# A four-layer graph network: z, y and x3 in x2's buffer, scores in the common PSUM banks, layer 3's nodes in the turns' order, bv added to v, whole products for the first four graphs

## The chip, the cores and the metric

One core of one Trainium2 chip runs the kernel. The metric is the device time of one execution in microseconds (us). Engines are named as the profile names them: PE (matrix products), PEld (its weight loads), DVE (vector engine), ACT (scalar engine), POOL (GpSimd), SP (the queue that issues most DMAs).

## The reference: what is computed

128 graphs `x[b]` of 128 nodes and 512 features pass four layers; all share one 128x128 adjacency matrix `adj`. Each layer ends in a residual sum and a layernorm over the features:

```
x1 = LN(x  + relu(max over nodes of adj @ x + b))            layer 0
h  = x1 @ W;  e = leaky_relu(s1_i + s2_j) * adj              layer 1, s1 and s2: h times two vectors
z  = softmax(e) @ h + beta * h
x2 = LN(x1 + elu(z))
x3 = LN(x2 + (adj @ x2) @ W2 + bias2)                        layer 2; the product is called y
q, k, v = x3 @ Wq + bq, x3 @ Wk + bk, x3 @ Wv + bv           layer 3, 8 heads of 64
out = LN(x3 + softmax(q k^T / 8 + mask) @ v)                 mask is -1e9 where adj is 0
```

Everything is float32.

## The kernel before: how the work is laid out

**Steps.** PE's work is cut into small steps per graph: `l0` (adj times x), `zT` (the attention matrix plus beta, times x1, transposed), `z` (times W), `yT` and `y` (the same for layer 2), `q`, `k`, `v`, `sc` (scores, one product per head) and `avT` (weights times v, transposed). The last six graphs (LATE) take another way at the end (`pT`, `av`), and the first four (EARLY) transpose on PE what the others transpose by DMA.

**Products in seven parts.** Two graphs (for z and y) or four (for q, k, v) are multiplied by a weight in seven products of blocks instead of eight, with sums of weight blocks (`weight_sums`, once) and differences of data blocks (`turned` for z and y, `token_sums` for q, k and v, on POOL). The seven steps of one product (`l1_seven`, `l2_seven`, `seven`) use three PSUM banks: *chain*, *first* and *pair*. Between the steps ACT copies the chain out into a temporary (`stz`, `sty`, `st`), and DVE adds it to what the other banks hold (`finish`; L610 for z, L721 for y, L878 for q, k and v). For y, POOL adds x2 to the temporary (L713).

**Turns.** A transpose of 128x128 blocks is done in `turn` (L373): the tile is written to device memory in four blocks, read back with blocks and rows exchanged, and DVE transposes 32x32 blocks (L393 in place for the softmax weights, L397 into another tile). The read gives the node order 32 x 4, so L397 writes with a step of four elements to restore it. x3 is turned for q, k and v (`turn_x`), the attention matrix (`turn_att`), the softmax weights (`turn_pr`) and the result of avT (`turn_o`). ACT's copy L1047 writes oT with a step of four as well, in both versions.

**Layer 3's last part.** `fetch` (L785) reads x3 back from device memory, in the copy that the turn wrote there, and POOL adds bv to it (L796). After turn_o, POOL multiplies by 1/denominator (L1060), adds x3 plus bv (L1061), and `last` makes the layernorm (L360, L362 on DVE, L365, L367, L369 on POOL, L371 on ACT) and writes the graph out.

**The order of the work.** `Plan` runs at build time: a model of the engines in which each piece of work has a cost in us written in the code, and marks for what must be done first. `run` takes PE's steps in the order of their `place` (turn of the graph plus an offset per step: l0 0, zT and z 2, yT and y 5, sc 14.5, av 17.5) among those that are ready in the model and find their buffers. The other engines' instructions are emitted when the model gives them to their engine, first ready first emitted. Every engine's queue, SP's included, then runs in the order of emission. HOP is the model's time from one engine to the next.

**Buffers.** x1 has five tiles of a graph, x2 four, xp four (for z, for y and x3, for the result), x3r one (for x3 read back), pr (the softmax weights) one. PSUM has eight banks: six under the tag mm for all products, and one tile of two banks, `sc`, for the scores. In `l3_scores` one DVE addition of mask and scores (L974) reads both banks.

Of the kernel before, what the change touches and what calls it, by code (L numbers as in the profile page):

```python
# [14 lines left out]
P = 128  # L15
# [4 lines left out]
HOP = 0.2  # L20


class Plan:

# [9 lines left out]
    def __init__(self, bufs):  # L34
        self.heap, self.count = [], 0
        self.engine = {}
        self.left = dict(bufs)
        self.parked = {tag: [] for tag in bufs}
        self.marks, self.waiting = {}, {}
        self.end = 0.0  # L40
# [35 lines left out]
    def events(self, until):  # L76
        while self.heap and self.heap[0][0] <= until:
# [13 lines left out]
            gen, (engine, us, landing) = item  # L91
            start = max(time, self.engine.get(engine, 0.0))
            self.engine[engine] = start + us
            self.end = start + us + landing + HOP
            self.resume(gen, self.end)
# [43 lines left out]
def kernel(  # L139
# [30 lines left out]
        "x0": 2, "x1": 5, "x2": 4, "x3r": 1, "xp": 4,  # L170
        "s2_bc": 2, "s2_row": 2, "e": 2, "pe": 2, "att": 1, "attT": 2, "zyT": 2, "Tzy": 1,
        "xTh": 3, "T": 1, "st": 3, "stzy": 2, "qTh": 3, "kTh": 3, "pr": 1, "pT": 1, "oT": 1,
        "turn1": 2, "turn4": 2,
    }
    ps_bufs = {"mm": 6, "sc": 1}
# [11 lines left out]
    def ps_tile(tag, name):  # L187
        shape = [P, 2, H // 2, P] if tag == "sc" else [P, 512]
        return psum.tile(shape, F32, tag=tag, name=name, bufs=ps_bufs[tag])
# [12 lines left out]
    def dve(us):  # L202
        return ("DVE", us - 0.09, 0.09)

    def act(us):
        return ("ACT", us - 0.1, 0.1)

    def pool(us):
        return ("POOL", us, 0.0)

    def sp(us, landing):
        return ("SP", us, landing)
# [12 lines left out]
    def load_w(w, name):  # L225
        return const.tile([P, NCC, C], F32, tag=name, name=name), w.rearrange("(c p) f -> p c f", p=P)

# [16 lines left out]
    for c in range(NCC):  # L244
# [9 lines left out]
        load_w(w, f"{n}_sb") for n, w in (("w2", w2), ("wq", wq), ("wk", wk), ("wv", wv))  # L254
# [3 lines left out]
    def later_loads():  # L258

        for us, dst, src in (  # L260
# [4 lines left out]
            yield act(0.16)  # L265
            nc.scalar.dma_start(out=dst, in_=src)
# [19 lines left out]
    nc.vector.tensor_scalar(mask, adj_sb, 0.0, NEG, ALU.is_equal, ALU.mult)  # L286
    mask_bc = mask.rearrange("p (b c) -> p b c", b=NQ).unsqueeze(1).to_broadcast([P, H, NQ, Q])
# [5 lines left out]
    def w1_a():  # L293

        yield sp(0.0, 6.5)
        for i in (1, 0):
# [18 lines left out]
            yield ("PE", 1.0, 0.0)  # L315
# [15 lines left out]
    def weight_sums(n, w):  # L331
# [4 lines left out]
        yield sp(0.0, {"z": 0.0, "y": 30.0, "q": 44.0, "k": 52.0, "v": 84.0}[n])  # L336
# [4 lines left out]
        if n == "z":  # L341
            yield ("mark", ("wa", 0))
# [14 lines left out]
    def layernorm(src, dst, name):  # L357
        yield dve(0.86)
        stats = small.tile([P, 6], F32, tag="stats", bufs=5, name=f"stats_{name}")
        nc.vector.bn_stats(stats, src)  # L360
        mv = small.tile([P, 2], F32, tag="mv", bufs=5, name=f"mv_{name}")
        nc.vector.bn_aggr(mv, stats)  # L362
        yield pool(1.09)
# [6 lines left out]
        yield act(0.82)  # L370
        nc.scalar.activation(dst, src, AF.Identity, bias=nmr, scale=rstd)  # L371

    def turn(src, tag, place, n, name, kept="turn_hbm{}"):  # L373
# [4 lines left out]

        kept = kept.format(n)
        d = yield from get_hbm(kept, [NQ, P, n * Q], f"turn_hbm_{name}")  # L380
        yield sp(0.35, {1: 4.0, 4: 5.5, 8: 5.5}[n])
        nc.sync.dma_start(out=d.rearrange("b p x -> p b x"), in_=src.rearrange("p b n r -> p b (n r)"))
        plan.give(tag)
        t = yield from get("pT" if place is None else f"turn{n}", [P, NQ, n, Q], f"turn_{name}")
# [4 lines left out]
        if kept.startswith("turn"):  # L389
            plan.give(kept)  # L390
        if place is None:
            yield dve(1.25)
            nc.vector.transpose(t.rearrange("p a n c -> p (a n c)"), t.rearrange("p a n c -> p (a n c)"))  # L393
            return t
        dst = yield from place()
        yield dve({1: 0.4, 4: 1.11}[n])
        nc.vector.transpose(dst.rearrange("p n (c a) -> p a n c", a=NQ), t)  # L397
        plan.give(f"turn{n}")
        return d
# [66 lines left out]
    def attention(b, s2_bc, tag):  # L466
# [26 lines left out]
        yield from turn(att.rearrange("p (b n c) -> p b n c", b=NQ, n=1), "att", lambda: made(s["attT"]), 1, f"att_{b}")  # L493
# [21 lines left out]
    def turned(n, b, ps):  # L515
# [10 lines left out]
        if j == 0:  # L526
            return
# [3 lines left out]
        for i, dst, x_, y_ in ((0, t[:, 0], b12, b11), (1, t[:, 1], b22, t[:, 0]), (2, b12, b22, b12), (3, t[:, 2], b21, t[:, 1])):  # L531
            yield pool(0.8)
# [20 lines left out]
    def pair_products(n, t):  # L553

        p, i = divmod(t, 7)
        d = pairs[n, p]
# [14 lines left out]
        if t == 7 * (B // 2) - 1:  # L571
# [3 lines left out]

    def pair_waits(n):
        def waits(t):
            p, i = divmod(t, 7)
            keys = [("sums", n)]
# [14 lines left out]
    def l1_seven(t):  # L594
# [3 lines left out]
        def half(j, r):  # L598
            return st[2 * p + j]["xp1"][:, r * HALF : (r + 1) * HALF]

        def temp():
            d["st", i] = yield from get("stzy", [P, HALF], f"stz_{p}_{i}")
            yield act(0.37)
# [3 lines left out]
        def finish(j, r, key):  # L607
            yield ("mark", ("z", p, key))
            yield dve(0.42)
# [4 lines left out]
        def take_xp(j):  # L614
            st[2 * p + j]["xp1"] = yield from get("xp", [P, C], f"xp1_{2 * p + j}")
# [3 lines left out]
        elif i == 1:  # L619
            yield from take_xp(0)  # L620
            yield from finish(0, 0, 0)
            plan.give("mm")
        elif i == 4:
            yield from temp()
            yield from take_xp(1)
            yield from finish(1, 1, 4)
        elif i == 5:
            yield ("mark", ("z", p, "C", 1, 1))
            yield act(0.37)
# [8 lines left out]
    def l1_rest(b):  # L638
        s = st[b]
        xp = s.pop("xp1")  # L640
        x2 = yield from get("x2", [P, C], f"x2_{b}")
        yield act(1.25)
        nc.scalar.activation(x2, xp, AF.Relu, scale=-1.0)
        nc.scalar.activation(x2, x2, AF.Exp, scale=-1.0)
        yield dve(1.5)
        nc.vector.scalar_tensor_tensor(xp, xp, 0.0, s.pop("x1"), ALU.max, ALU.add)  # L646
        nc.vector.scalar_tensor_tensor(xp, x2, -1.0, xp, ALU.add, ALU.add)  # L647
        plan.give("x1")
        yield from layernorm(xp, x2, f"1_{b}")
        plan.give("xp")  # L650
        s["x2"] = x2
# [21 lines left out]
    def token_sums(g):  # L673
# [8 lines left out]
        for i, dst, x_, y_ in ((0, t[:, 0], b12, b11), (1, t[:, 1], b22, t[:, 0]), (2, b12, b22, b12), (3, t[:, 2], b21, t[:, 1])):  # L682
            yield pool(1.4)
# [5 lines left out]
    def l2_seven(t):  # L689
# [3 lines left out]
        def half(j, r, tile):  # L693

            return st[2 * p + j][tile][:, r * HALF : (r + 1) * HALF]

        def xp_half(j, r):
            xp, b = st[2 * p + j]["xp2"], 2 * p + j
            if b < EARLY:
                return xp[:, r * HALF : (r + 1) * HALF]  # L700
# [489 lines left out]
```

## Time and profile before

| what | value |
|---|---|
| median of 3 runs | 2791.49 us (2790.95 to 2792.59) |
| the profiled execution | 2791.27 us |
| its span, first to last instruction | 2789.5 us |
| mean granted clock of PE | 0.988 |
| DMA | 392.58 MB in 459820 packets, 376624 of them under 2 KB |

The profile is one execution. A page lists the busy time of each engine; other views give windows of the span, a timeline, the waits, and groups of instructions by line. PE's matmuls are pipelined and their ends modelled, so the durations in the timeline overlap: the next start tells more than the duration. A wait is put down to the last of its releasers by the profile.

### The profile page before, as it was taken

To read this page: it belongs to the slowest core of one execution; us is meant where nothing else is said; L and a number is where in the kernel's file an instruction comes from. 1 tells how busy PE (TensorE), PEld (TensorE's weight loads), DVE (VectorE), ACT (ScalarE), POOL (GpSimd) and SP (SyncE) were. 2 spreads that over 40 slices of the span, in tenths; PEclk is the share of its full clock that TensorE was granted. 3 is DMA by queue.
4 is the path that set the end of the run, shared out by engine and by line. 5 is a ranking of instruction groups with operands and counts; after the bars stand their busy time and mean duration, and the time that the engine had idled before them with its cause. 6 is when DMAs were issued, how large, how long until landed. Compare 5 with 4: busy or idle time off the path is not lost.

```text
span 2789.5 us, 48120 instructions
## 1 busy us (share of the span) xinstructions
PE 2649.8 (95%) x15441; PEld 2228.5 (80%) x15441; DVE 2208.9 (79%) x4225; ACT 1828.3 (66%) x4893; POOL 1992.5 (71%) x2904
## 2 busy tenths in 40 slices
PE   5899999999999999999999999999999999999998
PEld 3688888888888888888888887888788887888887
DVE  6677888888778988888887878878778787888766
ACT  3566676676666667666676676666666666766655
POOL 5865778767768767677767777676686776777666
PEclk8999999999999999999999999999999999999998
DMA  3124355454444545454464444544544545445454
GB/s 119 44 58 136 118 162 153 129 178 136 145 149 141 154 142 156 140 165 143 133 184 132 150 145 139 157 146 131 150 147 140 158 139 152 141 137 160 129 158 134
DMA packets 459820, 392.58 MB, mean 141 GB/s; under 512 B 88752, under 2 KB 376624, under 8 KB 459568
## 3 DMA queue, kind: packets, MB, share of 16 engines
q1 hardware_dynamic: 456464, 383.74, 45.4%
q10 hardware_dynamic: 2976, 5.77, 0.6%
q8 instruction: 122, 2.00, 0.3%
q14 instruction: 130, 1.06, 0.1%
q0 software_dynamic: 128, 0.01, 0.0%
HBM read 218.17 MB, written 171.24 MB: 140 GB/s over the span
## 4 chain that ended last, share of the span: by engine, by line
PE 41%; DVE 24%; POOL 23%; issue 6%; DMA 3%; ACT 2%; SPq 0%; DVEq 0%; POOLq 0%; ACTq 0%
PE ps_z_chain L563 5%; POOL rstd L367 4%; PE ps_k_chain L843 4%; DVE stats L360 3%; PE ps_q_chain L843 3%; PE ps_k_pair L843 3%; DVE xp L646 3%; PE ps_z_pair L563 3%; PE ps_v_chain L843 3%; PE ps_y_chain L563 3%; DVE xp L647 2%; POOL xp L1061 2%; PE ps_q_pair L843 2%; POOL nmr L369 2%; DVE x L426 2%
## 5 line engine op out<-in xcount | busy, mean ns | idle before, releaser
L985 ACT ACTIVATE pr<-pr,nm 128x128 f32<-128x128 f32 x992 | 384.8, 392 | 50.6 <-DVE nm L980 49.3
L367 POOL TENSOR_TENSOR rstd<-ve,nhalf 128x1 f32<-128x1 f32 x512 | 307.2, 600 | 42.6
L365 POOL TENSOR_SCALAR ve<-mv 128x1 f32<-128x1 f32 x512 | 134.6, 263 | 273.2 <-DVE mv L362 225.5
L371 ACT ACTIVATE xp<-xp,nmr,rstd 128x512 f32<-128x512 f32 x256 | 207.9, 812 | 166.5 <-POOL nmr L369 164.2
L426 DVE SCALAR_TENSOR_TENSOR x<-x,wa_bc 128x512 f32<-128x512 f32 x256 | 228.6, 894 | 79.5 <-ACT x L371 78.2
L360 DVE BATCH_NORM_STATS2 stats<-xp 128x6 f32<-128x512 f32 x384 | 259.9, 677 | 37.4 <-POOL xp L1061 32.8
L1060 POOL TENSOR_TENSOR xp<-xp,rd 128x512 f32<-128x512 f32 x122 | 130.4, 1069 | 216.6 <-DVE xp L397 136.9
L796 POOL TENSOR_TENSOR x3r<-x3r,bv_bc 128x512 f32<-128x512 f32 x128 | 174.3, 1362 | 64.3 <-DMA x3r<-turn_hbm_x 58.8
L369 POOL TENSOR_SCALAR nmr<-mv,rstd 128x1 f32<-128x1 f32 x512 | 154.9, 303 | 53.0
L658 POOL TENSOR_TENSOR x<-x,bias_bc 128x512 f32<-128x512 f32 x128 | 167.3, 1308 | 29.1 <-PE ps_yT L665 27.5
L985 ACT ACTIVATION_READ_ACCUMULATOR pr<-pr,nm 128x1 f32 x976 | 185.4, 190 | 0.0
L713 POOL TENSOR_TENSOR sty<-sty,x 128x256 f32<-128x256 f32 x192 | 152.6, 796 | 37.9 <-ACT sty L709 37.8
L974 DVE TENSOR_TENSOR pr<-ps_sc,mask 128x1024 f32<-128x1024 f32 x124 | 150.2, 1211 | 28.5 <-PE ps_sc L952 24.6
L397 DVE STREAM_TRANSPOSE xTh<-turn_x 128x512 f32<-128x512 f32 x124 | 137.6, 1115 | 40.9 <-DMA turn_x<-turn_hbm_x 40.8
L1061 POOL TENSOR_TENSOR xp<-xp,x3r 128x512 f32<-128x512 f32 x122 | 160.2, 1313 | 9.6
L952 PE MATMUL ps_sc<-kTh,qTh 64*128 64x128 f32 x2048 | 149.0, 285 | 4.2 <-DVE pr L974 4.2
L393 DVE STREAM_TRANSPOSE turn_pr<-turn_pr 128x1024 f32<-128x1024 f32 x122 | 149.7, 1227 | 3.7 <-DMA turn_pr<-turn_hbm_pr 3.4
L563 PE MATMUL ps_y_chain<-sums_y,Ty 128*128 128x256 f32 x512 | 134.6, 386 | 16.4 <-POOL Ty L533 15.0
L665 PEld LDWEIGHTS ps_yT<-adjT,x 128*128 128x128 f32 x1024 | 134.6, 195 | 18.8 <-ACT x L371 11.4
L980 DVE TENSOR_REDUCE nm<-pr 128x8 f32<-128x1024 f32 x124 | 148.1, 1195 | 0.3
L542 PEld LDWEIGHTS ps_zT<-attT,x 128*128 128x128 f32 x1024 | 134.1, 193 | 16.8 <-issue 4.1
L1047 ACT COPY oT<-ps_av 128x512 f32<-128x512 f32 x122 | 131.6, 1079 | 22.7 <-PE ps_av L1035 18.5
(190 smaller groups left out, 7920.9 us busy)
## 6 DMA issues: line engine op xcount, KB each, us to landing
turn_hbm_pr<-pr SPq DMA_DIRECT2D x122, 512.0 KB
turn_pr<-turn_hbm_pr SPq DMA_DIRECT2D x122, 512.0 KB
x<-in_x_dram SPq DMA_DIRECT2D x128, 256.0 KB
out_dram<-xp SPq DMA_DIRECT2D x128, 256.0 KB
turn_hbm_x<-xp SPq DMA_DIRECT2D x124, 256.0 KB
turn_x<-turn_hbm_x SPq DMA_DIRECT2D x124, 256.0 KB
x3r<-turn_hbm_x SPq DMA_DIRECT2D x124, 256.0 KB
turn_hbm_o<-oT SPq DMA_DIRECT2D x122, 256.0 KB
```

The lines of the kernel that those rows point to most:

```text
L360: nc.vector.bn_stats(stats, src)
L367: nc.gpsimd.tensor_tensor(rstd, ve, nhalf, ALU.pow)
L369: nc.gpsimd.tensor_scalar(nmr, mv[:, 0:1], rstd, -1.0, ALU.mult, ALU.mult)
L371: nc.scalar.activation(dst, src, AF.Identity, bias=nmr, scale=rstd)
L426: nc.vector.scalar_tensor_tensor(xin_b, x1, 1.0, wa_bc[i], ALU.mult, ALU.mult, accum_out=col)
L563: nc.tensor.matmul(d[BANKS[i]], x_k[:, k], sums[n][w_i][:, k, :], start=fresh and k == 0, stop=k == 1, skip_group_check=not fresh,)
L658: nc.gpsimd.tensor_tensor(x2, x2, bias2_bc, ALU.add)
L713: nc.gpsimd.tensor_tensor(tmp, tmp, half(j, r, "x2"), ALU.add)
L796: nc.gpsimd.tensor_tensor(s["x3r"], s["x3r"], by_block(b, bv_bc), ALU.add)
L843: nc.tensor.matmul(ps[:, m, :], lhsT, rhs, start=fresh and m + k == 0, stop=m + k == 2, skip_group_check=not fresh)
L985: nc.scalar.activation(pr_h[:, i], pr_h[:, i], AF.Exp, bias=nm[:, i : i + 1], accum_out=None if late else den[:, i : i + 1])
L1061: nc.gpsimd.tensor_tensor(by_block(b, xp), by_block(b, xp), s.pop("x3r"), ALU.add)
```

## The change

- **One buffer for z, x2, y and x3.** z is written straight into the x2 tile, elu and the sum with x1 are made in x1's tile, the layernorm writes x2 back, y is added into it and x3 normalised in place. It is released when x3 is written to device memory (twice: once as it is, once in the turn). xp goes from four tiles to three and serves the result alone (and x3 of the first four graphs); x3r goes, and pr gets a second tile.
- **Scores in common banks.** mm gets all eight banks; scores take two of them, and mask and scores are added in two instructions, one for each bank.
- **The turns' order.** Layer 3 keeps the nodes in the order that the turn gives (32 x 4). The transposes of x3 and of the result write in a row; x3 is read back and the output written with permuted rows of 2 KB, the weights of q, k and v are loaded with permuted rows and the mask is permuted. In the last part the result stands by blocks, and the steps of four elements are in POOL's reading of x3 and in ACT's writing of the normalised rows.
- **bv goes to v.** POOL adds it to v's three temporaries of a group, DVE adds it at the group's last copy, which ACT did; L796 goes.
- **Whole products for four graphs.** z and y of the first four graphs are four products of 512 columns each, without blocks.
- **The planner.** Each engine has a queue by rank (0: work between the steps of a product; 1; 2: layer 3's last part), and an instruction is emitted when the model has it finished instead of when it begins. HOP goes from 0.2 to 0.35.

The core of the diff:

```diff
-HOP = 0.2
+HOP = 0.35
...
-            gen, (engine, us, landing) = item
-            start = max(time, self.engine.get(engine, 0.0))
-            self.engine[engine] = start + us
-            self.end = start + us + landing + HOP
-            self.resume(gen, self.end)
+            gen, want = item
+            engine = want[0]
+            if gen is not None:
+                heapq.heappush(self.queue.setdefault(engine, []), (want[3], time, self.count, gen, want[1], want[2]))
+                self.count += 1
+            if self.engine.get(engine, 0.0) <= time and self.queue.get(engine):
+                _, _, _, gen, us, landing = heapq.heappop(self.queue[engine])
+                self.engine[engine] = time + us
+                self.at(time + us, (None, want))
+                self.at(time + us + landing + HOP, gen)
+            elif gen is not None and self.engine.get(engine, 0.0) > time:
+                self.at(self.engine[engine], (None, want))
...
-        "x0": 2, "x1": 5, "x2": 4, "x3r": 1, "xp": 4,
+        "x0": 2, "x1": 5, "x2": 4, "xp": 3,
...
-    ps_bufs = {"mm": 6, "sc": 1}
+    ps_bufs = {"mm": 8}
...
+    def by_place(rows):
+        return rows.rearrange("(c a) f -> a c f", a=NQ)
...
-        yield dve({1: 0.4, 4: 1.11}[n])
-        nc.vector.transpose(dst.rearrange("p n (c a) -> p a n c", a=NQ), t)
+        yield dve({1: 0.4, 4: 0.72}[n], rank)
+        nc.vector.transpose(dst, t)
...
+    def whole_product(n, b):
+        p, j = divmod(b, 2)
+        ps = ps_tile("mm", f"ps_{n}_{b}")
+        w = {"z": w1_sb, "y": w2_sb}[n]
+        for c in range(NCC):
+            nc.tensor.matmul(ps, pairs[n, p]["T"][:, j, c], w[:, c, :], start=c == 0, stop=c == NCC - 1)
...
-        nc.vector.scalar_tensor_tensor(xp, xp, 0.0, s.pop("x1"), ALU.max, ALU.add)
-        nc.vector.scalar_tensor_tensor(xp, x2, -1.0, xp, ALU.add, ALU.add)
+        nc.vector.scalar_tensor_tensor(x1, z, 0.0, x1, ALU.max, ALU.add)
...
+        nc.vector.scalar_tensor_tensor(x1, x2, -1.0, x1, ALU.add, ALU.add)
...
+            yield sp(0.35, 2.5)
+            nc.sync.dma_start(out=s["x3_hbm"], in_=x3)
...
-            out=xb.rearrange("p (b x) -> p b x", b=NQ), in_=st[b].pop("x3_hbm").rearrange("b p x -> p b x")
-        )
...
-        yield pool(1.32)
-        nc.gpsimd.tensor_tensor(s["x3r"], s["x3r"], by_block(b, bv_bc), ALU.add)
+        nc.sync.dma_start(out=s["x3r"], in_=by_place(s.pop("x3_hbm")))
...
+                if n == "v":
+                    yield pool(1.32, 0)
+                    nc.gpsimd.tensor_tensor(t, t, bv_half(r), ALU.add)
+                    plan.mark((n, g, i, "b"))
...
+                if n == "v":
+                    yield dve(0.7, 0)
+                    nc.vector.tensor_tensor(out(0, 1), flat(ps), flat(bv_half(0)), ALU.add)
+                else:
+                    yield from copy(out(0, 1), 0)
...
-        yield dve(1.22)
-        nc.vector.tensor_tensor(
-            pr_h, ps.rearrange("p e f (b c) -> p (e f) b c", b=NQ), mask_bc, ALU.add
-        )
-        plan.give("sc")
+        for e in range(2):
+            yield dve(0.72)
+            nc.vector.tensor_tensor(
+                pr_h[:, NCC * e : NCC * (e + 1)], pss[e].rearrange("p f (b c) -> p f b c", b=NQ), mask_bc, ALU.add
+            )
+            plan.give("mm")
...
+        nc.gpsimd.tensor_tensor(o_m, o_m, xp.rearrange("p (m a) -> p a m", a=NQ), ALU.add)
+        yield from last(b, o_m, xp)
...
+    def last(b, src, xp, tag="xp"):
+        dst = xp if src is xp else xp.rearrange("p (m a) -> p a m", a=NQ)
...
-        nc.sync.dma_start(out=out[b], in_=xp)
+        nc.sync.dma_start(out=by_place(out[b]), in_=xp)
...
-        "z": (pair_place("z"), 0.88, pair_waits("z"), bank, l1_seven),
+        "z1": (place("z"), 3.45, lambda b: [("zT", b)], need("mm"), l1_whole),
+        "y1": (place("y"), 3.45, lambda b: [("yT", b)], need("mm"), l2_whole),
+        "z": (pair_place("z"), 0.88, pair_waits("z"), lambda t: {**bank(t), "x2+": 0 if t % 7 else 2}, l1_seven),
```

The last line lets a pair of z begin only when two x2 tiles are free in the model.

## The prediction

> **What bounds the kernel now.** I read the page's busy times first, then the windows of 100 us, then the matrix engine's (PE's) timeline, then its waits.
>
> ```profile
> span 2789.5 us, 48120 instructions
> PE 2649.8 (95%) x15441; PEld 2228.5 (80%) x15441; DVE 2208.9 (79%) x4225; ACT 1828.3 (66%) x4893; POOL 1992.5 (71%) x2904
> ```
>
> PE is busy for 95% of the span; no other engine is above 79%. By stage, in columns of length, busy time of PE, PEld, DVE, ACT and POOL, clock, DMA share and GB/s:
>
> ```profile
> 0.00:100.00 100.00, 60.03 (x205) 39.62 (x206) 70.51 (x151) 40.63 (x87) 60.32 (x86) 0.81 0.29 92
> 400.00:500.00 100.00, 99.15 (x596) 84.12 (x596) 84.00 (x163) 69.37 (x192) 73.03 (x104) 1.00 0.53 160
> 2300.00:2400.00 100.00, 95.15 (x562) 79.76 (x563) 77.02 (x150) 66.84 (x183) 71.79 (x107) 1.00 0.51 149
> ```
>
> The start loses most. Later windows issue between 545 and 596 matmul instructions (here 562 and 596), so even in the long middle the kernel is not always at its best rate. What that rate is, PE's timeline shows (start, duration, and what comes in how many instructions):
>
> ```profile
> 1401.22 1.89 PE L843 MATMUL ps_q_chain<-T,sums_q 128*128 128x256 f32 x8
> 1402.94 1.89 PE L843 MATMUL ps_k_chain<-T,sums_k 128*128 128x256 f32 x8
> 1404.67 1.05 PE L665 MATMUL ps_yT<-adjT,x 128*128 128x128 f32 x8
> 1405.56 1.89 PE L843 MATMUL ps_q_chain<-xTh,sums_q 128*128 128x256 f32 x8
> ...
> 1407.38 1.09 PE L1035 MATMUL ps_av<-turn_pr,va 128*64 128x128 f32 x16
> 1408.41 1.16 PE L952 MATMUL ps_sc<-kTh,qTh 64*128 64x128 f32 x16
> 1409.50 1.12 PE L410 MATMUL psA<-x,adjT 128*128 128x512 f32 x2
> ```
>
> The durations overlap, so a step's price is the distance from its start to the next one: 1.73 us for a q, k or v step, 0.89 for yT (zT the same), 1.03 for av, 1.09 for sc; elsewhere in that answer 0.86 for the layer-0 product (1435.76 to 1436.62) and 0.86 for a z or y step (1419.53 to 1420.39). One graph needs 0.86 + 2x0.89 + 7x0.86 (14 steps for two graphs) + 21x1.73/4 + 1.03 + 1.09 = 19.86 us. Counting the 32 "ps_q_first" steps of the timeline (one for four graphs), the second starts at 204.4, the 16th at 1380.7, the 30th at 2575.8: 21.01 us a graph in the first half, 21.34 in the second, 21.17 in all. So 1.31 us a graph is lost in the middle, about 150 us over the 115 graphs it holds. That and the start are all there is to gain. PE's waits name the causes (engine, line, waited for: total, times, longest):
>
> ```profile
> PE ps_y_pair L563 <- DVE xp L721: 26.6, 21, 2.3
> PE ps_y_chain L563 <- POOL Ty L533: 15.0, 17, 2.6
> PE ps_z_pair L563 <- POOL zT L533: 9.9, 11, 1.2
> PE ps_z_pair L563 <- DVE s_row L446: 9.0, 8, 1.6
> ```
>
> The first three and the smaller ones on Tz, yT, stz, st_v, sty, st_q and T come to 77 us for work between two steps of one product; 11 of these lie in the first 100 us, 66 behind.
>
> **The change, part by part.** Prices come from the groups by form (busy, mean ns, then idle before):
>
> ```profile
> L796 POOL TENSOR_TENSOR x3r<-x3r,bv_bc 128x512 f32<-128x512 f32 x128 | 174.3, 1362 | 64.3 <-DMA x3r<-turn_hbm_x 58.8 <-DMA x3r<-x_hbm 4.4 <-DVE xp L610 1.1
> L1061 POOL TENSOR_TENSOR xp<-xp,x3r 128x512 f32<-128x512 f32 x122 | 160.2, 1313 | 9.6
> L393 DVE STREAM_TRANSPOSE turn_pr<-turn_pr 128x1024 f32<-128x1024 f32 x122 | 149.7, 1227 | 3.7 <-DMA turn_pr<-turn_hbm_pr 3.4
> L397 DVE STREAM_TRANSPOSE xTh<-turn_x 128x512 f32<-128x512 f32 x124 | 137.6, 1115 | 40.9 <-DMA turn_x<-turn_hbm_x 40.8
> L1047 ACT COPY oT<-ps_av 128x512 f32<-128x512 f32 x122 | 131.6, 1079 | 22.7 <-PE ps_av L1035 18.5 <-issue 2.3 <-DMA x<-in_x_dram 1.5
> L523 ACT COPY zT<-ps_zT 128x512 f32<-128x512 f32 x128 | 73.7, 576 | 9.5 <-PE ps_zT L542 7.3
> ```
>
> *Nodes in the turns' order.* The transposes of L397 write in steps of four elements; 512 elements cost 1.11 us where 1024 written in a row (L393) cost 1.23. Without the steps one costs between 0.61 (half of L393) and 1.11; the 128-element one (0.40) gives a fixed part of about 0.16, so I take 0.69: (124+122) x 0.42 = 103 us off DVE. The steps move into layer 3's last part: ACT writes the result in steps of four, 122 times. ACT's copy with such a write takes 1.08 against 0.58 without, so +0.5 each, 61 us (bounds 0 and, doubling L371's 0.81, 99). POOL reads the residual in steps of four; no POOL row shows that, so it costs between nothing and a doubling of L1061's 1.31 (160 us); I take nothing, since L1061 has blocks of 32 today and costs no more than the plain L658 (1.31).
>
> Here the skill speaks against the change. The Trainium skill ("GPSIMD Engine Reference", section 7, Performance pitfalls for Q7 kernels) says that code reading SBUF in steps of more than 8 bytes takes about half as long again; by that, as an estimate, POOL gets 0.65 us x 122 = 80 us more. No row here has such a read. POOL would stand at 72% and the sum would not move, unless POOL's turn comes late in a product.
>
> *bv goes to v.* POOL loses L796 (174 us) and gains 96 additions of the same size (three a group, at L1061's price 126). The last v copy of a group moves from ACT (0.576) to DVE (L878, 0.675). A wait is added: the three finishing additions on DVE now wait for POOL, 1.3 us and two handovers, about 1.6. Behind them in DVE's queue stands whatever the plan put there, and PE's last v step waits for one of them: 0 to 32x1.6 = 51 us. I take 0, because av, sc and the other products stand between two v steps; with that cover gone it is the 51.
>
> *Scores in the common banks.* One DVE addition of 1.21 becomes two of 512 (0.675 by L878): +0.14x128 = 18 us of DVE. PE waited for scores' banks 4.2 us in all; the gain is two more banks for products, mostly free.
>
> *Whole products.* Four products of 512 columns (0.86 each) replace seven halves of a pair: 3.44 against 3.01 us a graph, +0.43 x 8 = **+3.4 us** of PE. In exchange the first four graphs have no differences, temporaries or weight sums to wait for: of PE's waits in the first 100 us the 11 named above go. What is late next is the latency of each graph's own chain (the layernorm, relu, exp), which still stands, and a clock of 0.57 to 0.83 between 20 and 60 us. Bounds -20 (the first q step now waits until 104.85) to +5; I take **-8**.
>
> *Engine totals.* DVE -103+18+22 = -63 (77%), ACT -18+61 = +43 (67%), POOL -48 and some 20 for the first graphs (69%). None is the bound, so these totals bring nothing by themselves.
>
> *DMAs.* x3 is written once more (124 x 256 KB = 32 MB on 392.58), its reading back goes from 512-byte to 2-KB pieces. The DMA share of about 0.5 covers it; if it didn't, up to 0.04 x 2789 would show. SP gets 124 more issues.
>
> *Ranks and emission.* The planner serves each engine by rank: work between two steps of a product first, layer 3's last part last. That aims at the 66 us. It also now emits an instruction when its model has it finished: on DVE, ACT and POOL this is the order of service, but on SP the order of landing. A turn's write (5.5 in the code) can land behind an output write (2.0) that is ready up to 3.5 us later, and SP's queue is in order (its longest wait, "SPq L382 <- DVE att L486", is 253.9 us already). So turns start 0 to 3.5 us later; layer 1's turn has the two graphs (42 us) between l0 and zT as cover. I take two thirds of the 66: **-45 us** (bounds 0 and -94, below), or 0.39 us a graph, which would put the middle at 20.8, a little under the first half's 21.01.
>
> *The tail.* After PE's last step near 2778 POOL still runs two L796 (2773.95 and 2779.03, 1.26 each) in the queue of the last layernorms. They go: **-2** (0 to -2.5).
>
> Sum: 2789.5 + 3.4 - 8 - 45 - 2 = 2738; the profiled run took 2791.27, 1.8 more than its span, so 2740. The median of the runs is 2791.49, 0.2 above the profiled one. A measurement of this kernel tells a difference from about 0.2% (5.6 us) on.
>
> **The rivals.**
> *More.* All the waits on promoted work go, with the time that PE's overlapping durations hide: the middle at 20.35, -0.82 x 115 = -94, 2690. For it: the window 400 to 500 already issues 596 instructions, 6% above that at 2300. Against: half of the loss has small and scattered causes.
> *Little.* The waits only change names (DVE first for one product is late for another, POOL's longer reads): a third or less of the 66, 2777.
> *Nothing.* The new SP order and the v wait give back what the ranks bring: 2791.
> *Slower, by x2.* Four x2 tiles now hold a graph from z's first half until x3's two writes; before, z, y and x3 had four xp besides. From the timeline, a pair's "z_first" to its last "y_pair" takes 54 to 75 us in most of the first 26 pairs, 99 to 116 afterwards; layernorm and write add some 8. Four tiles at 21.17 us a graph feed 84.7 us. If the hold can't be pressed under that, it decides: at 86.5 the period is 21.6, +0.45 x 115 = 52, and with the rest 2837. For it: the second half. Against: the first half ran at 21.01 with 62 to 83, and the long hold needed buffers that are no longer there, so z will simply begin later.
>
> **How the numbers follow.** Forecast 0.48 (its own range 2705 to 2770), more 0.17, little 0.14, nothing 0.07, slower by x2 0.14. Faster by over 0.2%: 0.79; within: 0.07; slower: 0.14. The range 2675 to 2800 leaves out most of the slower case and the lowest end of "more", 0.17 in all.
>
> **What would show it.** Right: q_first to q_first at 83 us or less; the waits on L721 and L533 a third of today's; the x and o transposes at 0.69; ACT's last normalisation at 1.3 for 122 of its calls; the first q step before 100 us. Wrong: PE or DVE waiting for x2 tiles (for a DMA write of x3, or "z" steps far behind "zT"), v's last step waiting for DVE, POOL above 75%.

## The result, and the profile after

The changed kernel takes 3046.57 us (median of 4 runs, 3044.99 to 3049.66), the kernel before 2792.04 in the same runs: ratio 1.0911, 95% interval 1.0892 to 1.093. A gain of 51 was predicted; 255 were lost. The profiled execution took 3047.13. The page of after:

```profile
span 3045.0 us, 48151 instructions
PE 2721.5 (89%) x15393; PEld 2259.6 (74%) x15393; DVE 2134.6 (70%) x4375; ACT 1851.3 (61%) x4847; POOL 1943.3 (64%) x2850
```

No engine has more to do: DVE and POOL fell as predicted, all shares fell. PE is now idle for 324 us instead of 140. Its busy time rose by 72 with 48 matmul instructions fewer, while the mean granted clock fell from 0.988 to 0.962; busy time multiplied by clock is 2618 us in both. The windows of after, with the columns as before:

```profile
0.00:100.00 100.00, 70.22 (x245) 40.72 (x246) 68.14 (x154) 44.36 (x90) 58.63 (x86) 0.92 0.44 107
400.00:500.00 100.00, 88.94 (x498) 74.18 (x496) 68.88 (x140) 60.15 (x164) 60.05 (x89) 0.97 0.47 142
2300.00:2400.00 100.00, 95.51 (x548) 79.98 (x547) 78.24 (x157) 65.65 (x174) 72.74 (x103) 1.00 0.50 156
```

The start is better: 245 instructions against 205, and the first "ps_q_first" step begins at 85.2 instead of 108.4. The middle is where the time went: 498 instructions against 596 in the second window. From the second to the 30th "ps_q_first" step (177.0 to 2774.5) a graph takes 23.19 us instead of 21.17; 2.02 x 112 = 226 of the 255. PE's waits in after, and below them DVE's:

```profile
PE ps_zT L567 <- DVE attT L419: 49.1, 23, 7.7
PE ps_y_pair L589 <- DVE x L768: 33.7, 16, 5.7
PE ps_y_chain L589 <- POOL Ty L558: 26.3, 17, 5.3
```

```profile
DVE xTh L419 <- DMA turn_x<-turn_hbm_x: 146.3, 55, 8.0
DVE turn_pr L415 <- DMA turn_pr<-turn_hbm_pr: 92.1, 33, 8.6
DVE turn_o L415 <- DMA turn_o<-turn_hbm_o: 45.9, 22, 5.8
DVE attT L419 <- DMA turn_att<-turn_hbm_att: 40.2, 18, 4.2
```

The first of PE's waits, for the turned attention matrix, was 1.1 us in before. DVE waits 324 us for turned tiles; in before these four waits have 40.8, 3.4, 7.8 and 3.5, together 56. The largest of them:

```profile
DVE xTh L397 <- DMA turn_x<-turn_hbm_x: 40.8, 25, 2.9
```

DVE's queue is in order, so what stands behind such a transpose (L768, an addition between two steps of a y product) is late as well. The chain of work that ended last says the same, first before, then after:

```profile
PE 41%; DVE 24%; POOL 23%; issue 6%; DMA 3%; ACT 2%; SPq 0%; DVEq 0%; POOLq 0%; ACTq 0%
```

```profile
PE 26%; DMA 25%; POOL 22%; DVE 14%; ACT 6%; issue 5%; SPq 2%; POOLq 0%; ACTq 0%; DVEq 0%
```

Transfers carry 25% of it instead of 3%. The DMA share of the two later windows did not rise (0.47 and 0.50), so by that column there is room. Two pieces of the chain (start, us, what):

```profile
1082.89 8.65 DMA turn_x<-turn_hbm_x
...
1097.43 3.94 DMA turn_hbm_o<-oT
```

The reading back of x3's turn takes 8.65 us here; its mean on the chain is 7.06 (34 times), in before 5.23 (3 times). The question of the experiments was who makes transfers slow or late.

### The profile page after: what moved, and what is told of

Same layout as the page of the kernel before. It is cut to its first block, busy times and chain, and to the rows that moved or that the text cites. A ratio compares the mean times of both kernels' runs of the same rounds, so it can differ in the third digit from the quotient of the medians.

```text
span 3045.0 us, 48151 instructions
## 1 busy us (share of the span) xinstructions
PE 2721.5 (89%) x15393; PEld 2259.6 (74%) x15393; DVE 2134.6 (70%) x4375; ACT 1851.3 (61%) x4847; POOL 1943.3 (64%) x2850
## 3 DMA queue, kind: packets, MB, share of 16 engines
q1 hardware_dynamic: 428564, 416.31, 45.3%
## 4 chain that ended last, share of the span: by engine, by line
PE 26%; DMA 25%; POOL 22%; DVE 14%; ACT 6%; issue 5%; SPq 2%; POOLq 0%; ACTq 0%; DVEq 0%
DMA turn_x<-turn_hbm_x 8%; DMA turn_pr<-turn_hbm_pr 4%; POOL rstd L392 4%; PE ps_z_chain L589 3%; POOL T L740 2%; POOL Ty L558 2%; PE ps_v_chain L898 2%; DVE stats L385 2%; DMA x3r<-x_hbm 2%; PE ps_q_chain L898 2%; POOL turn_o L1138 2%; DMA s_bc<-s_hbm 2%; DMA turn_att<-turn_hbm_att 2%; PE ps_zT L567 2%; POOL nmr L394 2%
## 5 line engine op out<-in xcount | busy, mean ns | idle before, releaser
L396 ACT ACTIVATE x<-x,nmr,rstd 128x512 f32<-128x512 f32 x384 | 311.4, 812 | 207.2 <-POOL nmr L394 191.9
L385 DVE BATCH_NORM_STATS2 stats<-x 128x6 f32<-128x512 f32 x384 | 258.4, 673 | 18.0 <-ACT x L440 17.1
L1138 POOL TENSOR_TENSOR turn_o<-turn_o,x3r 128x512 f32<-128x512 f32 x122 | 195.6, 1603 | 38.9 <-DMA x3r<-x_hbm 30.4
L396 ACT ACTIVATE x3r<-turn_o,nmr,rstd 128x512 f32<-128x512 f32 x122 | 161.6, 1327 | 79.0 <-POOL nmr L394 78.9
L567 PE MATMUL ps_zT<-attT,x 128*128 128x128 f32 x1024 | 149.4, 293 | 57.7 <-DVE attT L419 49.1
L932 POOL TENSOR_TENSOR st_v<-st_v,bv_bc 128x512 f32<-128x512 f32 x96 | 125.0, 1302 | 102.6 <-ACT st_v L918 102.6
L419 DVE STREAM_TRANSPOSE xTh<-turn_x 128x512 f32<-128x512 f32 x124 | 86.8, 701 | 146.6 <-DMA turn_x<-turn_hbm_x 146.3
L1044 DVE TENSOR_TENSOR pr<-ps_sc,mask 128x512 f32<-128x512 f32 x248 | 161.5, 676 | 26.7 <-PE ps_sc L1022 26.4
L1136 POOL TENSOR_TENSOR turn_o<-turn_o,rd 128x512 f32<-128x512 f32 x122 | 133.1, 1091 | 73.6 <-DVE turn_o L415 67.4
L432 PE MATMUL psA<-x,adjT 128*128 128x512 f32 x256 | 140.4, 633 | 15.9 <-DMA x<-in_x_dram 9.7
```

The costliest lines, as they stand in the source:

```text
L385: nc.vector.bn_stats(stats, src if flat is None else flat)
L567: nc.tensor.matmul(ps[:, c * P : (c + 1) * P], s["x1"][:, c * P : (c + 1) * P], attT, start=True, stop=True)
L1044: nc.vector.tensor_tensor(pr_h[:, NCC * e : NCC * (e + 1)], pss[e].rearrange("p f (b c) -> p f b c", b=NQ), mask_bc, ALU.add)
L1138: nc.gpsimd.tensor_tensor(o_m, o_m, xp.rearrange("p (m a) -> p a m", a=NQ), ALU.add)
```

## The experiments

Each was timed beside the kernel before, which stood at 2792.7 to 2793.7. A result is given in us and, in brackets, as the ratio to the kernel before with its 95% interval. The theories on record, by their letters: **S**, SP's queue in the order of landing makes transfers late; **X**, four x2 tiles are too few; **R**, the ranks starve layer 3's last part; **D**, the second write of x3; **V**, the wait for bv; **M**, the planner counts on transfers that are faster than the real ones, with no time to spare; **T**, the turns' order itself (second write, strided steps, turn4 held longer); **F**, found last, the permuted transfers use four of the 16 DMA engines.

### SP's order and the ranks

*e1_sp_start*: the changed kernel, SP's instructions emitted when the model begins them, as before.

```diff
-                self.at(time + us + landing + HOP, gen)
+                if engine == "SP":
+                    self.end = time + us + landing + HOP
+                    self.resume(gen, self.end)
+                else:
+                    self.at(time + us + landing + HOP, gen)
```

> The changed kernel, with one edit: SP's instructions are emitted when the model begins them, as before the change, instead of when it has them landed; the other engines as in the change. Theory S (SP's queue in the order of landing makes transfers start late): most of the loss goes, 2720 to 2800 us, and the waits of DVE for turned tiles (324 us for turn_x, turn_pr, turn_o and turn_att in the changed kernel, 56 before) fall to about 60. Theory X (four x2 tiles are too few): still 2980 to 3050, since the tiles are the same. Theory R (ranks put the wrong work first): still 2980 to 3050.

2902.69 (1.0395, 1.0376 to 1.0414). SP's order is worth 144 us here, yet 110 of the loss stay, and DVE still waits 249 us for turned tiles where S expected about 60.

*e2_before_sp_landing*: the reverse, the kernel before with SP's instructions emitted at landing.

```diff
-            self.resume(gen, self.end)
+            if engine == "SP":
+                self.at(self.end, gen)
+            else:
+                self.resume(gen, self.end)
```

> The kernel before, with one edit: SP's instructions alone are emitted when the model has them landed, as in the change. Theory S: slower than before by 5% to 10%, 2930 to 3070 us, with DVE waiting for turned tiles by 200 us or more. Theories X and R: within 1% of before (2765 to 2820), because buffers and ranks are those of before.

2823.5 (1.0114, 1.0097 to 1.0131). The same order costs 30 here and 144 there, and DVE waits 80 us for turned tiles instead of the 200 or more that S expected: something in the changed kernel makes it sensitive.

*e3_one_rank* (the changed kernel) and *e4_sp_start_one_rank* (e1_sp_start), each with all ranks equal:

```diff
-(want[3], time, self.count, gen, want[1], want[2])
+(0, time, self.count, gen, want[1], want[2])
```

> The changed kernel with all ranks equal, so each engine's queue is served first ready first; SP still in the order of landing. Theory R: back towards 2790, at most 2850. Theories S and X: 3000 to 3100, no better than the changed kernel or worse by up to 2%.

> Both edits: the changed kernel with SP emitted at the beginning and all ranks equal. Theory S: 2750 to 2830, within 2% of the run with ranks and SP at the beginning; the difference of the two is what ranks are worth (I expect ranks to gain 0 to 50 us). Theory R: no worse than 2790 here even if SP's order alone changes little. Theory X: still 2980 or more.

3073.18 (1.1005, 1.0988 to 1.1021) and 2904.29 (1.0403, 1.0387 to 1.0418). Ranks bring 27 under the order of landing and nothing under the other. R falls.

### Parts of the change by themselves

*e12_before_sharing* and *e13_before_sharing_five*: the kernel before with z, y and x3 in x2's buffer, four tiles of x2 and five.

```diff
-"x2": 4, "x3r": 1, "xp": 4,
+"x2": 4, "x3r": 1, "xp": 3,
...
-        nc.vector.scalar_tensor_tensor(xp, xp, 0.0, s.pop("x1"), ALU.max, ALU.add)
+        nc.vector.scalar_tensor_tensor(x1, z, 0.0, x1, ALU.max, ALU.add)
```

> The kernel before, with z, y and x3 in x2's buffer (four x2 tiles, xp three, features of q, k and v's weights permuted as in the change), nothing else. Theory X (four tiles are too few for z to x3): 2850 us or more, with DVE or PE held until a turn's write has read an x2 tile. Theory M (the loss comes from a plan that leaves no spare time for transfers): 2770 to 2830.

> The same with five x2 tiles. Theory X: clearly faster than with four, by 30 us or more. Theory M: within 20 us of the run with four.

2759.66 (0.9883, 0.9868 to 0.9897) and 2738.72 (0.9805, 0.9789 to 0.9822). Sharing is a gain with four tiles already; X falls. The fifth is worth 21.

*e8_before_bv_to_v* and *e15_sharing_bv*: bv added to v, in the kernel before and in the one with five tiles.

```diff
-        nc.gpsimd.tensor_tensor(s["x3r"], s["x3r"], by_block(b, bv_bc), ALU.add)
...
+                if n == "v":
+                    nc.gpsimd.tensor_tensor(t, t, bv_half(r), ALU.add)
```

> The kernel before, with bv added to v (three temporaries a group on POOL, the last copy on DVE) instead of to x3. Theory V: 2820 to 2880 us, with PE waiting for va behind v's steps. Theories D and M: 2770 to 2810, no loss.

> The kernel before with two parts of the change alone: z, y and x3 in x2's buffer (five tiles of x2) and bv added to v. Alone they gave 2739 (0.9805) and 2771 (0.9921). If they lift different waits, the gains add: 0.9805 x 0.9921 x 2793 = 2717. If both lift the same wait (POOL's and DVE's work between two steps of a product), the second brings little: 2730 to 2739. No theory expects it above 2745.

2771.15 (0.9921, 0.9906 to 0.9936) and 2754.74 (0.9865, 0.9845 to 0.9886). V falls: no wait of some 50 us appears. But the gains do not add: with sharing the same edit is 16 slower than without it, above what was expected. Each edit also makes the planner choose another order, so gains of 20 us are not properties of an edit alone.

*e6_before_extra_write*: the kernel before with one more write of x3, 256 KB, ahead of each of x3's turns.

```diff
+            extra = yield from get_hbm("extra_hbm", [P, n * P], f"extra_{name}")
+            yield sp(0.35, 2.5)
+            nc.sync.dma_start(out=extra, in_=src.rearrange("p b n r -> p (b n r)"))
```

> The kernel before, plus one write of x3 (256 KB, to a place nobody reads) ahead of each turn's write, so the same bytes as the change. Theory D: 2840 to 2900 us. Theory V: within 0.5% of before. Theory M: 2795 to 2830, a cost, but a smaller one, since before's plan has more spare time for a turn.

2778.62 (0.9948, 0.9933 to 0.9962). 32 MB more of plain writes cost nothing in this kernel, so D falls there; e24 below, which keeps the second write, agrees.

*e16_before_planner*: the kernel before with the planner of the change (queues, emission when finished, HOP 0.35), ranks equal.

```diff
-            self.resume(gen, self.end)
+            gen, want = item
...
+                self.at(time + us + landing + HOP, gen)
```

> The kernel before, with the new planner: a queue per engine, every instruction emitted when the model has it finished, HOP 0.35, all ranks equal. Theory S in its first form (the order alone costs the time): 2850 or more. Theory M: 2790 to 2850, since before's buffers and transfers leave the plan room.

2813.67 (1.0073, 1.0058 to 1.0088): 21 more than the kernel before, where e2's order of SP alone cost 30, so the planner's other parts cost nothing there.

### The wrong track: second write and costs

*e5_one_write*: e1_sp_start with x3 written once, in the turn, and read back from there in four parts (and three of the small tiles nm3 and den3).

```diff
             plan.at(plan.end, turn_x3(b))
+            return
...
-        nc.sync.dma_start(out=s["x3r"], in_=by_place(s.pop("x3_hbm")))
...
+            for a in range(NQ):
+                nc.sync.dma_start(out=s["x3r"][a * Q : (a + 1) * Q].rearrange("p (b x) -> p b x", b=NQ), in_=turned_x3[a])
```

> From the run with SP emitted at the beginning (2903 us): x3 is written once, by the turn, and read back from that copy in four pieces, as far as the traffic goes like before the change; the scores' small tiles (maxima, sums) are three instead of two. Theory D (the second write of x3, queued ahead of each turn's write, makes the turns land later: reads of turn_x on the chain of waits took 7.5 us on average there, 5.2 before the change): most of the remaining 110 us go, 2800 to 2850 us. Theory V (v's bias adds a wait that PE sees) and theory M (the plan counts on transfers faster than they are and has no spare buffers): 2880 to 2930, and SP's three more issues per graph may cost some.

2853.84 (1.0219, 1.0204 to 1.0234), 49 less. I put this down to the write, against e6; the edit also split the reading in four, and that was the point, as the last runs suggest.

*e11_costs* (e1_sp_start) and *e19_costs_landing* (the changed kernel): the planner's costs nearer the trace, and three small tiles.

```diff
-        yield sp(0.35, {1: 4.0, 4: 5.5, 8: 5.5}[n])
+        yield sp(0.35, {1: 6.0, 4: 6.5, 8: 6.5}[n])
...
-        yield sp(0.35, 5.0)
+        yield sp(0.35, 7.0)
```

> From the run with SP emitted at the beginning (2903 us): the plan's costs are set nearer to what the trace shows: landing of the turns' writes and reads 6.0 to 6.5 us instead of 4.0 to 5.5, reading x3 back 7.0, the s2 write 5.0, ACT's last normalisation 1.33, POOL's last part 2.7; small tiles of scores three. The work is the same, its order differs. Theory M: faster than 2903 by 30 us or more, because DVE stops standing at the head of its queue before a transfer that is still on its way. Theories D and V: no gain from it, 2890 to 2950.

> The changed kernel with the planner's costs corrected (landings of the turns, of x3's reading and of s2's write, ACT's and POOL's last steps; three of the small tiles), SP still in the order of landing. With SP in the order of beginning the same costs took 2903 to 2833, and SP's order alone took 3047 to 2903. If the two are separate causes, the costs bring the same here: 3047 - 70 = 2977. If they are one cause (transfers that come later than the plan counts on), the corrected counts cover most of SP's order as well: 2840 to 2900.

2833.37 (1.0145, 1.0128 to 1.0162), 69 less; but 3083.34 (1.1039, 1.1017 to 1.1061) under the order of landing, 37 more, where both readings on record expected less. M does not hold as a cause by itself; why longer counts hurt there is open.

*e17_costs_one_write*: both on e1_sp_start.

```diff
-        yield sp(0.35, 5.0)
+        yield sp(1.4 if b >= EARLY else 0.35, 7.0)
```

> The changed kernel with SP emitted at the beginning, the plan's costs nearer to the trace, and x3 written once, so both of the gains of the runs at 2833 and 2854 us together. If they are one and the same (late transfers), about 2820 to 2835; if they add, 2780 to 2800, and then little of the loss is left to explain.

2801.85 (1.0033, 1.0023 to 1.0044). Three corrections added up to 245, and still without the gains that sharing alone brings.

### The turns' order under the old planner

*e20_turns_order*: the kernel with sharing (five tiles) and the turns' order; planner, banks and bv as before. *e21_turns_bv_whole*: with bv to v and the whole products too.

```diff
-        nc.vector.transpose(dst.rearrange("p n (c a) -> p a n c", a=NQ), t)
+        nc.vector.transpose(dst, t)
...
+        nc.sync.dma_start(out=s["x3r"], in_=by_place(s.pop("x3_hbm")))
...
+        nc.sync.dma_start(out=by_place(out[b]), in_=xp)
```

> The kernel before with sharing (five tiles of x2, 2739 by itself) and the turns' order: x3 written twice, transposes written in a row, ACT's last normalisation and POOL's reading of x3 in steps of four; the planner, the scores' banks, the single pr tile and bv stay as before (no x3r tile, as in the change, and three of the small tiles nm3 and den3). Theory M+S (the loss came from the planner's order, which sends transfers late and counts them too short): the turns' order costs little here, as the extra write alone did, and 2715 to 2750 results. Theory T (the turns' order itself costs, by its second write, the strided steps of ACT and POOL at the end of a graph, or the turn4 tiles held longer): 2790 to 2840.

> The run with the turns' order, with bv to v and the whole products of four graphs besides: all of the change except its planner, the scores' common banks and the second pr tile, and with five tiles of x2. Theory M+S: 2690 to 2730, faster than before, since bv and the sharing bring what they bring alone and the start is 23 earlier. Theory T: 2770 to 2820. If it stands at 2690 to 2730, what is missing of the changed kernel at its best version so far (2802) lies in the planner and the common banks alone.

2987.13 (1.0695, 1.067 to 1.072) and 2961.27 (1.0605, 1.0587 to 1.0623). The loss came with the turns' order alone, 248 over the same kernel without it (2738.72), with the old planner and banks. That leads to the transfers themselves. The time of each from its issue on SP to the last update of its semaphore is worked out from the trace's semaphore records (eight semaphores, used in turn). Medians in us over all transfers of a kind, e20 being the first of these two runs, e23 and e24 the two that follow:

```
transfer             before  after   e20   e23   e24
out<-result            2.27   7.08  6.94  1.72  1.73     each of four parts in e23, e24
x3r<-memory            3.72   6.79  6.49  2.65  2.59     each of four parts in e23, e24
turn_x<-turn_hbm_x     3.48   6.53  4.61  3.18  2.89
turn_hbm_x<-x3         2.30   4.07  4.05  3.62  3.37
turn_pr<-turn_hbm_pr   3.92   4.60  4.92  4.23  4.00
turn_hbm_pr<-pr        3.07   5.01  4.95  3.69  3.75
turn_hbm_att<-att      1.79   3.55  3.52  2.51  2.47
```

The two permuted transfers carry the same 256 KB as before, in rows of 2 KB, and land three times and nearly twice as late. A transfer of such a size otherwise leaves 16 updates, but these two leave one at 0.98 us and four at the end (medians 5.9 to 7.0). And in after, turn_x's own 16 split: the medians of the first twelve run from 3.15 to 3.91 us, of the last four from 5.46 to 6.53 (before: 2.58 to 3.48 without a step). This fits a permuted transfer that runs on four engines and holds up there what the others bring. The pattern that `by_place` makes has an outer dimension of four (a of "a c f").

The Trainium skill ("DMA: Bandwidth & Descriptors", section "Why a DMA increments its semaphore by 16 and not by 1") has this rule: a copy issued from SP runs on the largest number of engines, up to 16, that divides the slowest dimension of both access patterns, and the issuer writes the missing updates at once. The one early update and the four late ones are what it describes. In e20 itself the transfers were not split, so how much of its 248 is theirs is not shown.

### The same transfers in four parts

*e23_spread*: the changed kernel; *e24_spread_sp_start*: e1_sp_start; in each the two transfers are four of 32 rows, so that the outer dimension is 32.

```diff
-        nc.sync.dma_start(out=s["x3r"], in_=by_place(s.pop("x3_hbm")))
+        rows = s.pop("x3_hbm").rearrange("(c a) f -> a c f", a=NQ)
+        for a in range(NQ):
+            nc.sync.dma_start(out=s["x3r"][a * Q : (a + 1) * Q], in_=rows[a])
...
-        nc.sync.dma_start(out=by_place(out[b]), in_=xp)
+        rows = out[b].rearrange("(c a) f -> a c f", a=NQ)
+        for a in range(NQ):
+            nc.sync.dma_start(out=rows[a], in_=xp[a * Q : (a + 1) * Q])
```

> The changed kernel with one difference: each of the two transfers with permuted rows (x3 read back, the graph written out) is issued as four transfers of 32 rows instead of one with an outer dimension of four; bytes, rows and order stay. Theory F (the permuted transfers run on four of the 16 DMA engines, so they land after 7.2 and 8.8 us instead of 2.3 and 3.7, and hold up every other transfer on these four): the two land within some 2.5 and 4.5 us, the last four landings of a turn no longer lag behind the first twelve, and 2740 to 2860 results; what stays above 2740 is what SP's order costs by itself (1.1% in the kernel before). Theory M (plan's too short counts and SP's order are the cause, and slow transfers only its sign) and theory T (the strided steps of ACT and POOL): 3030 to 3060, or later, since SP issues six transfers more for each graph.

> The run with SP's instructions emitted when the model begins them (2903), with the same two transfers in four parts. Theory F: 2700 to 2790, because writing x3 once with the read in four parts already gave 2854, and by the kernel before an extra write costs nothing; what is left against the other run of this pair is SP's order by itself: 20 to 60 if it costs what it cost in the kernel before (1.1%), 140 if it is a cause of its own in the changed kernel. Theories M and T: 2880 to 2920.

2823.14 (1.011, 1.0093 to 1.0127) and 2738.54 (0.9807, 0.9793 to 0.9822). The same bytes and rows with six more issues a graph take back 223 and 164 us; each part leaves its 16 updates, and turn_x's last four no longer lag (2.92 to 3.18 behind 2.53 to 2.88 in e23). From the first issue of the four parts to the last landing the write takes 3.1 us and the read 3.8 (medians in e24), against 7.1 and 6.8 in after; the 8.8 of the expectation is not the median of all reads. F is shown. The table of the four:

| | SP at landing | SP at beginning |
|---|---|---|
| permuted transfers whole | 3046.57 (after) | 2902.69 |
| in four parts | 2823.14 | 2738.54 |

The page of e24, then its chain and DVE's waits for turned tiles:

```profile
span 2737.1 us, 49283 instructions
PE 2628.8 (96%) x15393; PEld 2210.7 (81%) x15393; DVE 2142.9 (78%) x4375; ACT 1849.7 (68%) x4847; POOL 1950.6 (71%) x2850
```

```profile
PE 55%; POOL 22%; DVE 11%; ACT 4%; issue 4%; DMA 3%; SPq 0%; POOLq 0%; ACTq 0%; DVEq 0%
```

```profile
DVE xTh L423 <- DMA turn_x<-turn_hbm_x: 27.5, 25, 4.6
DVE turn_pr L419 <- DMA turn_pr<-turn_hbm_pr: 9.1, 9, 2.4
DVE attT L423 <- DMA turn_att<-turn_hbm_att: 5.9, 5, 2.9
DVE turn_o L419 <- DMA turn_o<-turn_hbm_o: 5.1, 8, 1.1
```

Transfers are back at 3% of the chain and the waits at 48, while the DMA share rose (0.59 in the window from 400 to 500): more bytes a second and fewer waits. SP's order by itself is 85 us here. DVE's waits for turned tiles are 157 in e23 against those 48, longer for all four kinds: turn_x 59.6, turn_pr 58.7, turn_o 25.5 and turn_att 12.8. Of SP's own waits, the one for an output that is not ready to be written is the longer under the order of landing, first e23, then e24; the third line is the same wait in before:

```profile
SPq L1151 <- ACT x3r L396: 212.4, 61, 15.3
```

```profile
SPq L1155 <- ACT x3r L400: 116.6, 51, 9.1
```

```profile
SPq L1068 <- ACT xp L371: 200.6, 87, 14.1
```

While SP's queue stands at an output write, the turns emitted behind it wait too. But the sum of this wait alone does not give the cost: before stands there for 201 us and after for only 107. Which entry of the queue makes the turns late, and why the order costs 85 here and 30 in the kernel before, was not settled; six more issues a graph stand in that queue.

The two best versions, e24 and e13 (sharing with five tiles alone), stand level at 2738.5 and 2738.7. The fifth x2 tile, or better costs, on e24 was not tried.

## Why the prediction was wrong

Two steps failed.

**"DMAs": "The DMA share of about 0.5 covers it".** This weighed bytes and packets and never asked on how many engines a transfer runs. The share is a mean over 16 engines. In after (an estimate): 45.3% x 16 x 3045 = 22,070 us of engine time, of which the 256 permuted transfers have 128 packets each at 0.105 us, the mean of 2-KB packets: 3,440, all on the same four engines. With the rest evenly spread, four engines are busy for (1164 + 860) / 3045 = 66%, the other twelve for 38%, and turns come in bursts. The step counted nothing, with an upper bound of 0.04 x 2789 = 112; measured were 223 (164 with SP's order of before). The extra write itself was priced right, at nothing (e6).

**"Ranks and emission": "So turns start 0 to 3.5 us later; layer 1's turn has the two graphs (42 us) between l0 and zT as cover".** SP's order measured 85 us without the first fault and 144 with it. Cover for layer 1's turn is no cover for the others: under this order DVE waits longer for all four kinds of turned tile, those of x3 and of the softmax weights most (157 us in e23 against 48 in e24). The prediction named the delay and let it go after looking at one of the four turns. How the delay comes about in SP's queue stays open. The 253.9 us that the prediction calls SP's longest wait is the sum of 75 waits, the longest of them 10.3.

Without these two, e24 is the change as it was priced, at 2738.54 against the forecast 2740. That the totals agree so closely is in part luck, since several terms were off or right for another reason, and sharing alone (e13) takes the same time. Its steps:

- *Middle.* 20.8 us a graph forecast; 20.83 in e24 (180.4 to 2513.6, 112 graphs). PE's waits on L721 and L533, 57 in all in before, are 26 in e24 (13.1, 7.1, 4.8 and 1.4) where a third was forecast. But ranks brought 2 us in e1 (against e4) and 27 under the order of landing (e3), and were not tested on e24: the forecast -45 was about right in size, and its reason is not borne out. Sharing, priced at nothing, gives 33 to 54 alone.
- *Whole products.* The first "ps_q_first" step came at 85.2 in after and 88.7 in e24 instead of 108.4: the bound of -20, not the -8 taken.
- *Prices of the turns' order.* These rows of after answer to those of before:

```profile
L419 DVE STREAM_TRANSPOSE xTh<-turn_x 128x512 f32<-128x512 f32 x124 | 86.8, 701 | 146.6 <-DMA turn_x<-turn_hbm_x 146.3
L396 ACT ACTIVATE x3r<-turn_o,nmr,rstd 128x512 f32<-128x512 f32 x122 | 161.6, 1327 | 79.0 <-POOL nmr L394 78.9
L1138 POOL TENSOR_TENSOR turn_o<-turn_o,x3r 128x512 f32<-128x512 f32 x122 | 195.6, 1603 | 38.9 <-DMA x3r<-x_hbm 30.4
L932 POOL TENSOR_TENSOR st_v<-st_v,bv_bc 128x512 f32<-128x512 f32 x96 | 125.0, 1302 | 102.6 <-ACT st_v L918 102.6
```

  The transpose takes 0.70 (0.69 forecast), ACT 0.81 + 0.52 (+0.5 forecast). POOL's strided reading adds 0.29 to 1.31, where I took nothing and the estimate from the Trainium skill's "GPSIMD Engine Reference", section 7, was 0.65; 35 us in all.
- *bv.* 96 additions at 1.30 as forecast; PE's largest wait for DVE's additions to v sums to 9.6 us in after and 3.3 in e24, against the 51 of lost cover.
- *Rivals.* "Slower, by x2" was on the right side for the wrong reason: with four tiles the sharing is a gain in the kernel before (e12). Nor does its reading "99 to 116 afterwards" come out of the trace of before: from its "z_first" to its last "y_pair" a pair takes 54 to 83 us, all 64 pairs counted. "Nothing" held half of the truth, that SP's order eats the gains, at a third of its price.

## What to carry to other kernels

When a change alters a transfer's access pattern, look at its outer dimension, not only at its bytes and rows: with an outer dimension of four it ran on four of 16 DMA engines, and the mean DMA share did not show it. Compare each transfer's time from issue to landing before and after; one that lands two or three times as late can also delay those beside it. In an in-order issue queue, price a delay for everything that stands behind it.

## What the runs showed of the hardware

- A transfer of 256 KB on four engines landed after 7.1 us (write) and 6.8 us (read), on sixteen, in before, after 2.3 and 3.7; with two such transfers in 23 us the turns' transfers landed 0.7 to 3.1 us later (the table's rows; medians).
- 32 MB of further writes over sixteen engines cost nothing (2778.62 against 2793); e24 moves 425 MB at 155 GB/s with the waits of before.
- More idle time of PE went with a lower granted clock, so lost time showed twice, as idle time and as slower products: after and e24 issue the same 15,393 matmul instructions, busy for 2721.5 us at a granted clock of 0.962 (PE idle for 10.6% of the span) and for 2628.8 at 0.992 (4.0%). Over the traces of all 20 kernels busy time multiplied by clock stays between 2608 and 2640 us.
- ACT's strided write (steps of four elements) took 1.33 us against 0.81, POOL's strided read 1.60 against 1.31, DVE's transpose 1.11 with a strided write against 0.70.
